# Attention block in float32: another order of the first two pairs, and the bias shift through W1 by column groups

## The chip, the cores and the metric

The kernel runs on one core of one Trainium2 chip, in one launch. Times are device microseconds of that core, medians of several runs; a profile is one further execution, recorded instruction by instruction. Engine names in the text: PE (TensorE), DVE (VectorE), ACT (ScalarE), POOL (GpSimd), SP (the queue that only issues DMAs); PEq, ACTq, SPq are the instruction queues of an engine.

## The reference

A cross-attention block of a transformer, all in float32, for 128 sequences of 128 tokens, 256 features, 16 heads of 16, with an FFN of 1024:

```python
q = query @ Wq + bq;  k = context @ Wk + bk;  v = context @ Wv + bv     # heads of 16
scores = q k^T / 4;  scores[j >= i] = -1e30                              # strictly below the diagonal
attn = softmax(scores);  attn[row 0] = 0
x = layer_norm(query + (attn v) @ Wo + bo, ln1_g, ln1_b)
out = layer_norm(x + relu(x @ W1 + b1) @ W2 + b2, ln2_g, ln2_b)
```

The kernel folds the first norm's gain and shift into the FFN: with x1 the norm without gain and shift, x @ W1 + b1 = x1 @ (g1 * W1) + (b1 + ln1_b @ W1).

## The kernel before, in words

Two sequences are a *pair*; there are 64 pairs. For each the kernel transposes x and the context (`tokens`, a DVE 32x32 transpose of blocks that the load DMAs have already put in place), projects them (`queries`, `keys`, `values`, PE with eviction on ACT), and computes the scores in two parts. "High" (hi = 1) is the second half of the query rows against all 128 keys, "low" (hi = 0) the first half against 64 keys. Each part goes through `mask` (DVE, PSUM to `sm`), `maximum` (DVE reduce `nmx`, then POOL subtracts, L355), `exponential` (ACT), and `sums` (DVE reduce and reciprocal, then POOL multiplies, L376).

The weights are then transposed for the product with the values: `turn` (DVE 32x32 transposes into `tb`) and `bring` (sixteen DMAs tb to pT that exchange the blocks), or `turn_on_pe` (four PE transposes and an ACT copy per piece). `weigh` and `context` give the attention's output (ACT copies it to cxT), `attention_out` multiplies by Wo, `attention_sum`, `attention_stats`, `norm1` make x1. `turn_x1` transposes x1 (DVE, then four DMAs to DRAM, x1t, and one back, x1T); `turn_x1_on_pe` does it with PE and ACT. `hidden` is the first FFN product with ReLU on ACT, `second` the other, `second_sum`, `stats`, `norm2`, `finish`, `store` the last norm and the output. `add_bo`, `residual1`, `scale_and_shift` and `finish` run on POOL.

The order of instructions on every engine is written by hand: each engine executes its instructions in the order of the Python calls, and tiles of a pool hold a writer back until the former readers are done (PSUM: four single banks and two pairs). Nothing is reordered by a scheduler.

The program has four parts: an opening for pairs 0 and 1; steps p = 2 to 6, each in one order with a `plan` that says which halves of the FFN of earlier pairs run where; the usual step `steady(p)` from p = 7 to 62; and an end. In step p the pair p goes through its softmax, pair p-1 through `weigh` to x1, pair p+1 is projected, and the FFN runs for pairs p-2 (`hidden`) and p-3 (`second`). In the usual step the sixteen `bring` DMAs are issued half by SP, half by ACT between the pieces of `hidden`.

Three folds are made on the chip once: `fold_values` (bv @ Wo + bo), `fold_norm1` with `add_b1` (ln1_b @ W1 + b1, a column per 128 hidden units, `b1e_c`), and `scale_w1` (W1 times the gain). `fold_norm1` before is 32 matmuls with 128x128 of W1 as weights and one moving column (`ps_b`, L564).

Of the kernel before, what the change touches and what calls it, by code (L numbers as in the profile page):

```python
# [13 lines left out]
P = 128  # L14
# [5 lines left out]
def tile_cross_attention_block(  # L20
# [107 lines left out]
    c_first = const.tile([P, 2, D], F32, tag="c_first", name="c_first")  # L128
    nc.sync.dma_start(c_first, c[0:2].rearrange("b p d -> p b d"))
# [3 lines left out]
    wv = weight(Wv, "wv")  # L133
    power = const.tile([P, 2, 1], F32, tag="power", name="power")
# [7 lines left out]
    load([1])  # L142
# [6 lines left out]
    load([2, 3], "x")  # L149
    w1 = weight(W1, "w1")  # L150
    load([2, 3], "c")
    load_tokens(0, slice(2, 4))
# [4 lines left out]
    load_tokens(1)  # L157
    g2_r = row(ln2_g, "g2_r")
# [157 lines left out]
    def scores(p, hi):  # L316

        st = states[p]
        n = P if hi else HP
        sps = [pair(f"pss{hi}_{p}_{t}") for t in range(2)]  # L320
        for m in range(KC):
            for s in range(2):
                first = s * P
                for r in range(NS):
                    strip = slice(32 * r, 32 * r + 32)
                    nc.tensor.matmul(  # L326
                        sps[r // 2][
                            s * HP : (s + 1) * HP, r % 2, m * 2 * n : (m + 1) * 2 * n
                        ].rearrange("p (e j) -> p e j", e=2),
                        st["qT"][strip, m, first + hi * HP : first + hi * HP + HP],  # L330
                        st["kT"][strip, m, :, first : first + n],
                        start=True, stop=True,
                    )
# [221 lines left out]

    ps_b1 = None

    def fold_norm1():

        nonlocal ps_b1  # L560
        ps = ps_b1 = bank("ps_b1")
        for f in range(FC):
            for k in range(KC):
                nc.tensor.matmul(  # L564
                    ps[:, f : f + 1], w1[:, k, f * P : (f + 1) * P], be1_c[:, k : k + 1],
                    start=(k == 0), stop=(k == KC - 1),
                )

    def add_b1():
        nc.vector.tensor_tensor(b1e_c, ps_b1[:, :FC], b1_c, ALU.add)  # L570
# [7 lines left out]
    def fold_values():  # L578

        ps = bank("ps_bv")  # L580
        for k in range(KC):
            nc.tensor.matmul(
                ps[:, :D], bvw[:, k, :], wo[:, k, :], start=(k == 0), stop=(k == KC - 1)
            )
        nc.vector.scalar_tensor_tensor(bov_r, ps[:, :D], live, bo_r, ALU.mult, ALU.add)
# [14 lines left out]
    def turn_x1_on_pe(p):  # L600
# [6 lines left out]
        for k in range(KC):  # L607
            nc.scalar.copy(st["x1T"][:, :, :, k, :], pt[:, k])  # L608

    def hidden(p, fs, between=None):  # L610
# [3 lines left out]
        for f in fs[::2]:  # L614
# [25 lines left out]

    def second_alone(p, s):

        st = states[p]
        if "t2" not in st:
            st["t2"] = ffn.tile([P, 2, D], F32, tag="t2", name=f"t2_{p}")
        py = bank(f"py_{p}_{s}")
        for f in range(FC):
            nc.tensor.matmul(  # L648
                py[:, :D], st["hT"][:, f, s * P : (s + 1) * P], w2[:, f, :],
                start=(f == 0), stop=(f == FC - 1),  # L650
            )
        st["py", s] = py

    def sum_alone(p, s):
        st = states[p]
        nc.vector.tensor_tensor(
            st["t2"][:, s], st.pop(("py", s))[:, :D], st["x1b"][:, s], ALU.add
        )
# [17 lines left out]
    for which, first in (("x", tokens_of[0][:, 0:2]), ("c", c_first)):  # L676
# [16 lines left out]
    keys(0)  # L693

    def feed(units):
        for what, p, part in units:
            if what == "hidden":
                hidden(p, range(part * FC // 2, (part + 1) * FC // 2))
            elif p in alone:
                second_alone(p, part)  # L700
            else:
                second(p, part)

    def sum_up(units):

        done = []
        for what, p, part in units:
            if what == "second":
                if p in alone:
                    sum_alone(p, part)  # L710
                elif part == 1:
                    second_sum(p)
                if part == 1:
                    done.append(p)
        return done

    alone = (1, 2)

    def both(what, p):
        return [(what, p, 0), (what, p, 1)]  # L720


    scores(0, 1)
    mask(0, 1, 0)
    maximum(0, 1, ONE)
    values(0)
    mask(0, 1, 1)
    maximum(0, 1, TWO)
    scores(0, 0)
    tokens(1, "x")  # L730
    exponential(0, 1, ONE)
    values_out(0)
    queries(1)
    sums(0, 1, ONE)
    mask(0, 0, 0)
    mask(0, 0, 1)
    tokens(1, "c")
    exponential(0, 1, TWO)
    maximum(0, 0, ALL)
    keys(1)  # L740
    sums(0, 1, TWO)
    values(1)
    exponential(0, 0, ALL)
    turn_on_pe(0, 1, range(2))
    values_out(1)
    sums(0, 0, ALL)
    scores(1, 1)
    mask(1, 1, 0)
    maximum(1, 1, ONE)
    fold_values()  # L750
    turn_on_pe(0, 1, range(2, 4))
    turn_on_pe(0, 0, range(2))
    add_bo(0)
    mask(1, 1, 1)
    maximum(1, 1, TWO)
    tokens(2, "x")
# [3 lines left out]
    fold_norm1()  # L760
    mask(1, 0, 0)
    mask(1, 0, 1)
    exponential(1, 1, ONE)
# [3 lines left out]
    scale_w1()  # L767
    tokens(2, "c")
    add_b1()
# [3 lines left out]
    sums(1, 1, ONE)  # L773
    norm1(0)
    sums(1, 1, TWO)
    exponential(1, 0, ALL)
    keys(2)
    values(2)
    turn_x1_on_pe(0)
    values_out(2)  # L780
    sums(1, 0, ALL)
    for which in "xc":
        tokens(3, which)
    nc.gpsimd.tensor_tensor(be1b_r, be1_r, b2_r, ALU.add)
    residual1(0)
    add_bo(1)
    load([4, 5])
    load_tokens(2)
    add_bo(2)
    feed([("hidden", 0, 0)])  # L790
    turn_on_pe(1, 1, range(4))
    turn_on_pe(1, 0, range(2))

    plan = {
        2: ([("hidden", 0, 1)], both("second", 0), [("hidden", 1, 0)]),
        3: ([("hidden", 1, 1)], [("second", 1, 0)], [("second", 1, 1)]),
        4: ([("hidden", 2, 0)], [("hidden", 2, 1)], [("second", 2, 0)]),
        5: ([("second", 2, 1)], [("hidden", 3, 0)], [("hidden", 3, 1)]),  # L800
    }
# [7 lines left out]
    def steady(p):  # L809

        nonlocal waiting, late
# [3 lines left out]
        second(p - 3, 0)  # L815
# [3 lines left out]
        second(p - 3, 1)  # L819
        if p + 2 < NP:  # L820
            tokens(p + 2, "c")
        sums(p, 1, ONE)
        exponential(p, 1, TWO)
        summed = late + sum_up(both("second", p - 3))
# [6 lines left out]
        queries(p + 1)  # L831
# [6 lines left out]
        for q in waiting:  # L838
            finish(q)
        attention_out(p - 1)  # L840
# [3 lines left out]
        if p + 2 < NP:  # L844
            tokens(p + 2, "x")
        turn(p, 0, 0)
# [3 lines left out]
        turn_x1(p - 1)  # L850
        values(p + 1)
# [11 lines left out]
        def share(f):  # L863
            nonlocal at
            n = 0 if f == 0 else NS if f == FC - 2 else NS // 2
# [3 lines left out]
        hidden(p - 2, range(FC), share)  # L869
        late = []  # L870
# [4 lines left out]
    waiting, late = [], []  # L875
    for p in range(2, NP):
        soon, end = p + 1 < NP, p == NP - 1
        first, then, finally_ = plan.get(
            p, ([("second", p - 3, 0)], [("second", p - 3, 1)], both("hidden", p - 2))
        )  # L880
        load_ahead(p)
        if p > 6 and not end:
            steady(p)
            continue
        scores(p, 1)
        mask(p, 1, 0)
        maximum(p, 1, ONE)
        feed(first)
        mask(p, 1, 1)
        maximum(p, 1, TWO)  # L890
        scores(p, 0)
        mask(p, 0, 0)
        mask(p, 0, 1)
        exponential(p, 1, ONE)
        maximum(p, 0, ALL)
        exponential(p, 1, TWO)
        feed(then)
        sums(p, 1, ONE)
        sums(p, 1, TWO)
        summed = late + sum_up(first + then)  # L900
        exponential(p, 0, ALL)
        sums(p, 0, ALL)
        for q in waiting:
            finish(q)
        weigh(p - 1)
        context(p - 1)
        if soon:
            queries(p + 1)
        attention_out(p - 1)
        if not end:  # L910
            turn(p, 1, 0)
            turn(p, 1, 1)
            turn(p, 0, 0)
            bring(p, nc.sync, range(NS * NS))
        attention_sum(p - 1)
        attention_stats(p - 1)
        if soon:
            keys(p + 1)
        if p + 2 < NP:
            for which in "xc":  # L920
                tokens(p + 2, which)
        norm1(p - 1)
        if p > 4:
            turn_x1(p - 1)
        if soon:
            values(p + 1)
            values_out(p + 1)
        for q in waiting:
            store(q)
        if p == 2:  # L930
            turn_x1_on_pe(p - 1)
        residual1(p - 1)
        for q in summed:
            stats(q, states[q]["t2"], 2)
        if soon:
            add_bo(p + 1)
        for q in summed:
            scale_and_shift(q)
        feed(finally_)
        if end:  # L940
            turn_on_pe(p, 1, range(4))
        if p in (3, 4):
            turn_x1_on_pe(p - 1)
        late = sum_up(finally_)
        for q in summed:
            norm2(q)
        waiting = summed
# [88 lines left out]
```

## Time and profile before

| | us |
|---|---|
| median of 3 runs (lowest, highest) | 1605.69 (1603.98, 1606.11) |
| profiled execution | 1604.26 |
| its span on the core | 1602.5 |
| PE busy in the span | 1581.9 (99%) |
| DVE, POOL, ACT busy | 1368.0, 1281.9, 758.9 |

The profiled execution's own time is 1.8 us above its span. Busy time of PE is that of pipelined matmuls whose ends are modelled, so 99% says that PE is nearly always occupied, not that it is at its peak. Durations in the text come from this one execution.

### The profile page before, as it was taken

How to read it: one execution, taken by the hardware profiler on the slowest of the kernel's cores; microseconds unless marked ns; L12 is line 12 of the kernel's file. 1: busy time of each engine (PE TensorE's matmuls, PEld its weight loads, DVE VectorE, ACT ScalarE, POOL GpSimd, SP SyncE). 2: the span in 40 equal slices, each digit the busy share in tenths (PEclk: the TensorE clock that was granted, in tenths of full speed). 3: DMA queues.
4: the chain of work that ended last, by engine and by line, in shares of the span. 5: the costliest groups of instructions: out<-in, count | busy, mean ns of one | idle time of the engine just before them, and what ended most of it. 6: DMA issues, size and time to landing. Idle time of an engine off the chain costs nothing.

```text
span 1602.5 us, 41277 instructions
## 1 busy us (share of the span) xinstructions
PE 1581.9 (99%) x16532; PEld 1333.4 (83%) x16532; DVE 1368.0 (85%) x1988; ACT 758.9 (47%) x1500; POOL 1281.9 (80%) x1105
## 2 busy tenths in 40 slices
PE   7999999999999999999999999999999999999998
PEld 6788888888888888888888888888888888888887
DVE  5789898898888988988988888888889889889862
ACT  4544444544444545444544444444444455455442
POOL 5688888888888888888888888878888888888882
PEclk9999999999999999999999999999999999999999
DMA  7455656666565566565565565565655665654430
GB/s 179 72 117 126 147 128 141 132 134 146 128 147 132 128 147 146 121 152 133 122 156 138 117 148 129 131 150 128 144 134 133 141 145 127 149 132 107 117 83 27
DMA packets 479999, 208.80 MB, mean 130 GB/s; under 512 B 352064, under 2 KB 448320, under 8 KB 479808
## 3 DMA queue, kind: packets, MB, share of 16 engines
q1 hardware_dynamic: 373360, 137.17, 39.3%
q10 hardware_dynamic: 106448, 68.99, 16.6%
q8 instruction: 131, 2.15, 0.6%
q14 instruction: 60, 0.49, 0.1%
HBM read 69.48 MB, written 32.24 MB: 63 GB/s over the span
## 4 chain that ended last, share of the span: by engine, by line
PE 94%; DVE 3%; POOL 1%; ACT 1%; issue 1%; DMA 1%; ACTq 0%; SPq 0%; POOLq 0%; DVEq 0%
PE ph L618 27%; PE py L636 26%; PE pq L260 7%; PE po L465 7%; PE pk L260 7%; PE pv L292 6%; PE pss L326 6%; PE pc L446 3%; PE pc L436 2%; DVE sm L343 1%; DVE nmx L354 1%; PE py L648 1%; PE ptp L419 0%; POOL sm L376 0%; ACT kT L282 0%
## 5 line engine op out<-in xcount | busy, mean ns | idle before, releaser
L355 POOL TENSOR_TENSOR sm<-sm,nmx 128x1024 f32<-128x1024 f32 x192 | 364.2, 1897 | 135.9 <-DVE nmx L354 135.8
L618 PE MATMUL ph<-x1T,w 128*128 128x256 f32 x2048 | 454.1, 379 | 2.1 <-ACT x1T L608 2.1
L636 PE MATMUL py<-w,hT 128*128 128x256 f32 x1952 | 438.9, 382 | 0.5 <-ACT hT L624 0.5
L618 PEld LDWEIGHTS ph<-x1T,w 128*128 128x128 f32 x2048 | 388.5, 190 | 56.8 <-ACT x1T L608 3.2
L636 PEld LDWEIGHTS py<-w,hT 128*128 128x128 f32 x1952 | 365.6, 190 | 71.1 <-issue 15.5
L376 POOL TENSOR_TENSOR sm<-sm,rs 128x1024 f32<-128x1024 f32 x192 | 364.0, 1898 | 71.7 <-DVE rs L375 68.8
L624 ACT ACTIVATE hT<-ph,b1e_c 128x256 f32<-128x256 f32 x512 | 212.6, 471 | 205.2 <-PE ph L618 127.6
L343 DVE TENSOR_TENSOR sm<-pss,neg 128x1024 f32<-128x1024 f32 (+1 forms) x256 | 235.4, 940 | 78.3 <-PE pss L326 77.1
L362 ACT ACTIVATE sm<-sm 128x1024 f32<-128x1024 f32 x192 | 202.2, 1055 | 206.7 <-POOL sm L355 206.3
L374 DVE TENSOR_REDUCE su<-sm 128x8 f32<-128x1024 f32 (+1 forms) x192 | 233.5, 1216 | 51.1 <-ACT sm L362 47.7
L389 DVE STREAM_TRANSPOSE tb<-sm 128x1024 f32<-128x1024 f32 x183 | 219.8, 1227 | 28.3 <-POOL sm L376 27.7
L354 DVE TENSOR_REDUCE nmx<-sm 128x8 f32<-128x1024 f32 (+1 forms) x192 | 234.2, 1220 | 6.6
L534 ACT ACTIVATE t<-t,nb,sd 128x256 f32<-128x256 f32 x124 | 67.7, 593 | 181.8 <-DMA pT<-tb 110.7
L282 ACT ACTIVATE kT<-pk,bkh,half 128x256 f32<-128x256 f32 x256 | 122.6, 558 | 15.5 <-PE pk L260 15.5
L260 PE MATMUL pq<-xT,wq 128*128 128x256 f32 x512 | 127.9, 393 | 1.2 <-DVE xT L245 1.2
L465 PE MATMUL po<-wo,cxT 128*128 128x256 f32 x512 | 122.9, 383 | 1.4 <-ACT cxT L458 1.4
L260 PE MATMUL pk<-cT,wk 128*128 128x256 f32 x512 | 121.1, 379 | 1.3 <-DVE cT L245 1.3
L326 PE MATMUL pss<-kT,qT 32*64 32x256 f32 (+1 forms) x4096 | 118.1, 334 | 3.0 <-DVE sm L343 1.7
L292 PE MATMUL pv<-wv,cT 128*128 128x256 f32 x512 | 121.1, 379 | 0.0
L271 ACT ACTIVATE qT<-pq,bqs_c 128x256 f32<-128x256 f32 x128 | 53.6, 470 | 122.4 <-PE pq L260 122.4
L513 POOL TENSOR_TENSOR x1b<-x,g_r 128x512 f32<-128x512 f32 x64 | 81.7, 1276 | 36.9 <-DVE x L505 36.9
L465 PEld LDWEIGHTS po<-wo,cxT 128*128 128x128 f32 x512 | 98.2, 192 | 15.1 <-ACT cxT L458 1.6
(86 smaller groups left out, 1780.9 us busy)
## 6 DMA issues: line engine op xcount, KB each, us to landing
pT<-tb SPq DMA_DIRECT2D x528, 96.0 KB, 2.9
pT<-tb ACTq DMA_DIRECT2D x448, 96.0 KB, 2.8
out_dram<-t ACTq DMA_DIRECT2D x63, 256.0 KB, 2.5
xb<-in_x_dram SPq DMA_DIRECT2D x124, 128.0 KB, 4.4
cb<-in_ctx_dram SPq DMA_DIRECT2D x124, 128.0 KB, 4.4
x<-in_x_dram SPq DMA_DIRECT2D x31, 512.0 KB, 5.0
x1t<-tbx SPq DMA_DIRECT2D x236, 64.0 KB, 2.2
x1T<-x1t SPq DMA_DIRECT2D x59, 256.0 KB, 3.3
```

The source lines that it names most:

```text
L260: nc.tensor.matmul(ps[:, m * TP : (m + 1) * TP], w[:, k, m * P : (m + 1) * P], src[:, k, :], start=(k == 0), stop=(k == KC - 1),)
L292: nc.tensor.matmul(pv[:, s * D : (s + 1) * D], st["cT"][:, k, s * P : (s + 1) * P], wv[:, k, :], start=(k == 0), stop=(k == KC - 1),)
L326: nc.tensor.matmul(sps[r // 2][s * HP : (s + 1) * HP, r % 2, m * 2 * n : (m + 1) * 2 * n].rearrange("p (e j) -> p e j", e=2), st["qT"][str ...
L343: nc.vector.tensor_tensor(st["sm", hi][:, part, :].rearrange("p (r n) j -> p r n j", r=2), st["sps", hi][t][:, :, : 4 * n].rearrange("p r ...
L354: nc.vector.tensor_reduce(nmx[:, part], sm[:, part, :], AX.X, ALU.max, negate=True)
L355: nc.gpsimd.tensor_tensor(sm[:, part, :], sm[:, part, :], nmx[:, part, None].to_broadcast([P, part.stop - part.start, n]), ALU.add,)
L374: nc.vector.tensor_reduce(su, sm[:, part, :], AX.X, ALU.add)
L376: nc.gpsimd.tensor_tensor(sm[:, part, :], sm[:, part, :], rs[:, :, None].to_broadcast([P, part.stop - part.start, n]), ALU.mult,)
L389: nc.vector.transpose(st["tb"][:, :, at : at + 256].rearrange("p j (n a) -> p n j a", a=32), st["sm", hi].rearrange("p h j -> p (h j)")[:, ...
L465: nc.tensor.matmul(po[:, s * D : (s + 1) * D], cxT[:, k, s, :], wo[:, k, :], start=(k == 0), stop=(k == KC - 1),)
L618: nc.tensor.matmul(ph[:, i * TP : (i + 1) * TP].rearrange("p (s i a) -> p s i a", s=2, a=32), w1[:, k, (f + i) * P : (f + i + 1) * P], st[ ...
L636: nc.tensor.matmul(st["py"][:, s * D : (s + 1) * D], st["hT"][:, f, s * P : (s + 1) * P], w2[:, f, :], start=(f == 0), stop=(f == FC - 1),)
```

## The change

The opening and the first steps are written in another order.

- Pair 1 is no longer loaded as blocks (`load([1])`) and turned by DVE. Its x and context come as plain tokens, are transposed by PE after `scores(0, 1)`, and copied by ACT. `load([2, 3])` is issued earlier, `load([4, 5])` in the opening.
- `keys(0)` is written out with one bank per 128 outputs; ACT evicts the first, DVE the second.
- The order of calls in the opening differs throughout. `fold_norm1`, the transposes of pair 1's weights and the first half of `hidden(0)` come after `scores(2, 1)` instead of before it, so the high scores tile `sm1` has two buffers.
- `fold_norm1` uses ln1_b as weights of one column and W1 as the moving operand: eight matmuls of 256 columns, four column groups at PSUM partitions 0, 32, 64 and 96. Its result lies along four rows, which ACT copies to `b1s`; `add_b1` brings them into columns with eight DMAs on SP and adds b1 on POOL. This happens in step 2, after `turn_x1(1)`. Until then pair 0 goes through the FFN with the unscaled W1: gain and shift are applied to its x1T by ACT, and `scale_w1` follows `hidden(0)`.
- The usual step, now `step(p)`, runs from p = 2 on. In step 2 the FFN part is `hidden(0)` alone. Pairs 1, 2 and 3 turn x1 with `turn_x1`. The `plan`, `feed`, `second_alone` and `sum_alone` are gone. The end is the same.

```diff
+    load_tokens(0, slice(2, 4))
+    nc.sync.dma_start(c_first[:, 2:4], c[2:4].rearrange("b p d -> p b d"))
-    load([1])
...
-        st["sm", hi] = soft.tile([P, H, n], F32, tag=f"sm{hi}", name=f"sm{hi}_{p}")
+        st["sm", hi] = soft.tile(
+            [P, H, n], F32, tag=f"sm{hi}", name=f"sm{hi}_{p}", bufs=1 + hi
+        )
...
     def fold_norm1():
+        ps = bank("ps_b1")
+        n = DFF // NS
+        for k in range(KC):
+            for j in range(NS):
+                nc.tensor.matmul(
+                    ps[32 * j : 32 * j + 1, :n], be1_c[:, k : k + 1],
+                    w1[:, k, j * n : (j + 1) * n], start=(k == 0), stop=(k == KC - 1),
+                )
+        for j in range(NS):
+            at = slice(32 * j, 32 * j + 1)
+            nc.scalar.copy(b1s[at], ps[at, :n])
+
+    def add_b1():
         for f in range(FC):
-            for k in range(KC):
-                nc.tensor.matmul(
-                    ps[:, f : f + 1], w1[:, k, f * P : (f + 1) * P], be1_c[:, k : k + 1],
-                    start=(k == 0), stop=(k == KC - 1),
-                )
-    def add_b1():
-        nc.vector.tensor_tensor(b1e_c, ps_b1[:, :FC], b1_c, ALU.add)
+            j, u = f // 2, f % 2
+            nc.sync.dma_start(
+                b1e_c[:, f : f + 1], b1s[32 * j : 32 * j + 1, u * P : (u + 1) * P]
+            )
+        nc.gpsimd.tensor_tensor(b1e_c, b1e_c, b1_c, ALU.add)
...
     def turn_x1_on_pe(p):
...
+            if p == 0:
+                nc.scalar.activation(
+                    st["x1T"][:, :, :, k, :], pt[:, k], AF.Identity,
+                    bias=be1_c[:, k : k + 1], scale=g1_c[:, k : k + 1],
+                )
...
     def hidden(p, fs, between=None):
...
-                    bias=b1e_c[:, f + i : f + i + 1], scale=1.0,
+                    bias=(b1e_c if p else b1_c)[:, f + i : f + i + 1], scale=1.0,
...
+    def step(p):
+        if p > 2:
+            load_ahead(p)
         scores(p, 1)
         mask(p, 1, 0)
         maximum(p, 1, ONE)
+        if p > 2:
+            second(p - 3, 0)
+        else:
+            turn_x1_on_pe(0)
+            fold_norm1()
+            turn_on_pe(1, 1, range(4))
+            hidden(0, range(FC // 2))
+            turn_on_pe(1, 0, range(2))
         mask(p, 1, 1)
         maximum(p, 1, TWO)
         exponential(p, 1, ONE)
...
+        else:
+            for which in "xc":
+                tokens(3, which)
+            add_bo(1)
+            load_ahead(2)
+            load_tokens(2)
         sums(p, 1, ONE)
         exponential(p, 1, TWO)
         sums(p, 1, TWO)
         weigh(p - 1)
         context(p - 1)
         scores(p, 0)
         queries(p + 1)
         mask(p, 0, 0)
         mask(p, 0, 1)
         maximum(p, 0, ALL)
         exponential(p, 0, ALL)
         turn(p, 1, 0)
         turn(p, 1, 1)
...
+        if p == 2:
+            nc.gpsimd.tensor_tensor(be1b_r, be1_r, b2_r, ALU.add)
+            residual1(0)
+            add_bo(2)
         attention_out(p - 1)
         attention_sum(p - 1)
         sums(p, 0, ALL)
         attention_stats(p - 1)
...
         turn(p, 0, 0)
         bring(p, nc.sync, range(NS * NS // 2))
         keys(p + 1)
         norm1(p - 1)
         turn_x1(p - 1)
+        if p == 2:
+            add_b1()
         values(p + 1)
         values_out(p + 1)
...
         add_bo(p + 1)
         residual1(p - 1)
...
+        hidden(p - 2, range(0 if p > 2 else FC // 2, FC), share)
+        if p == 2:
+            scale_w1()
```

More of the change, by code (lines that the diff above doesn't have):

```diff
@@ L127, in tile_cross_attention_block @@
     wq = weight(Wq, "wq")
-    c_first = const.tile([P, 2, D], F32, tag="c_first", name="c_first")
-    nc.sync.dma_start(c_first, c[0:2].rearrange("b p d -> p b d"))
+    c_first = const.tile([P, 4, D], F32, tag="c_first", name="c_first")
+    nc.sync.dma_start(c_first[:, 0:2], c[0:2].rearrange("b p d -> p b d"))
     bq_c = column(bq, "bq_c")
@@ L148, in tile_cross_attention_block @@
     be1_c = chunks(ln1_b, "be1_c")
-    load([2, 3], "x")
+    load([2, 3])
     w1 = weight(W1, "w1")
-    load([2, 3], "c")
-    load_tokens(0, slice(2, 4))
     g1_r = row(ln1_g, "g1_r")
@@ L157, in tile_cross_attention_block @@
     load_tokens(1)
+    load([4, 5])
     g2_r = row(ln2_g, "g2_r")
@@ L554, in tile_cross_attention_block @@
     b1e_c = const.tile([P, FC], F32, tag="b1e_c", name="b1e_c")
-    ps_b1 = None
+    b1s = const.tile([P, DFF // NS], F32, tag="b1s", name="b1s")
     def fold_norm1():
-        nonlocal ps_b1
-        ps = ps_b1 = bank("ps_b1")
-        for f in range(FC):
-            for k in range(KC):
-                nc.tensor.matmul(
-                    ps[:, f : f + 1], w1[:, k, f * P : (f + 1) * P], be1_c[:, k : k + 1],
-                    start=(k == 0), stop=(k == KC - 1),
-                )
-    def add_b1():
-        nc.vector.tensor_tensor(b1e_c, ps_b1[:, :FC], b1_c, ALU.add)
+        ps = bank("ps_b1")
[10 more added lines that the diff above has]
+    def add_b1():
+        for f in range(FC):
+            j, u = f // 2, f % 2
[3 more added lines that the diff above has]
+        nc.gpsimd.tensor_tensor(b1e_c, b1e_c, b1_c, ALU.add)
     def scale_w1():
@@ L584, in fold_values, with add_values @@
             )
+        return ps
+    def add_values(ps):
         nc.vector.scalar_tensor_tensor(bov_r, ps[:, :D], live, bo_r, ALU.mult, ALU.add)
@@ L607, in turn_x1_on_pe @@
         for k in range(KC):
-            nc.scalar.copy(st["x1T"][:, :, :, k, :], pt[:, k])
+            if p == 0:
[4 more added lines that the diff above has]
+            else:
+                nc.scalar.copy(st["x1T"][:, :, :, k, :], pt[:, k])
     def hidden(p, fs, between=None):
@@ L639, in second @@
             )
[L641 to L658, printed above, removed]
     def second_sum(p):
@@ L675, in tile_cross_attention_block @@
     states[0] = {}
-    for which, first in (("x", tokens_of[0][:, 0:2]), ("c", c_first)):
+    for which, first in (("x", tokens_of[0][:, 0:2]), ("c", c_first[:, 0:2])):
         st = states[0]
@@ L692, in tile_cross_attention_block @@
     queries(0)
[L693 to L700, printed above, removed]
-            else:
[L702 to L715, printed above, removed]
@@ L717, in tile_cross_attention_block @@
-    alone = (1, 2)
-    def both(what, p):
-        return [(what, p, 0), (what, p, 1)]
-    scores(0, 1)
+    st["kT"] = proj.tile([P, KC, 2, TP], F32, tag="kT", name="kT_0")
+    for m in range(KC):
+        pk = bank(f"pk_0_{m}")
+        for k in range(KC):
+            nc.tensor.matmul(
+                pk[:, :TP], wk[:, k, m * P : (m + 1) * P], st["cT"][:, k, :],
+                start=(k == 0), stop=(k == KC - 1),
+            )
+        for e in range(2):
+            if m == 0:
+                nc.scalar.activation(
+                    st["kT"][:, m, e, :], pk[:, :TP], AF.Identity,
+                    bias=bkh[:, m, e : e + 1], scale=half[:, e : e + 1],
+                )
+            else:
+                nc.vector.tensor_scalar(
+                    st["kT"][:, m, e, :], pk[:, :TP], half[:, e : e + 1],
+                    bkh[:, m, e : e + 1], ALU.mult, ALU.add,
+                )
@@ L724, in tile_cross_attention_block @@
+    scores(0, 1)
+    states[1] = {}
+    for which, first in (("x", tokens_of[0][:, 2:4]), ("c", c_first[:, 2:4])):
+        st = states[1]
+        st[which + "T"] = proj.tile([P, KC, TP], F32, tag=which + "T", name=f"{which}T_1")
+        pt = transposed(first, f"pt{which}_1")
+        nc.scalar.copy(st[which + "T"].rearrange("p k i -> p (k i)"), pt)
+    values(0)
+    values_out(0)
     mask(0, 1, 0)
     maximum(0, 1, ONE)
-    values(0)
     mask(0, 1, 1)
     maximum(0, 1, TWO)
+    exponential(0, 1, ONE)
@@ L729, in tile_cross_attention_block @@
+    queries(1)
     scores(0, 0)
[L730 to L734, printed above, removed]
     mask(0, 0, 0)
     mask(0, 0, 1)
-    tokens(1, "c")
+    maximum(0, 0, ALL)
     exponential(0, 1, TWO)
-    maximum(0, 0, ALL)
+    sums(0, 1, ONE)
     keys(1)
     sums(0, 1, TWO)
+    exponential(0, 0, ALL)
     values(1)
-    exponential(0, 0, ALL)
-    turn_on_pe(0, 1, range(2))
-    values_out(1)
+    ps_bv = fold_values()
     sums(0, 0, ALL)
@@ L748, in tile_cross_attention_block @@
     mask(1, 1, 0)
+    add_values(ps_bv)
     maximum(1, 1, ONE)
-    fold_values()
+    turn_on_pe(0, 1, range(2))
+    values_out(1)
     turn_on_pe(0, 1, range(2, 4))
-    turn_on_pe(0, 0, range(2))
-    add_bo(0)
     mask(1, 1, 1)
     maximum(1, 1, TWO)
-    tokens(2, "x")
+    add_bo(0)
+    turn_on_pe(0, 0, range(2))
+    for which in "xc":
+        tokens(2, which)
     weigh(0)
@@ L759, in tile_cross_attention_block @@
     scores(1, 0)
-    fold_norm1()
+    exponential(1, 1, ONE)
     mask(1, 0, 0)
     mask(1, 0, 1)
-    exponential(1, 1, ONE)
     maximum(1, 0, ALL)
@@ L766, in tile_cross_attention_block @@
     exponential(1, 1, TWO)
-    scale_w1()
-    tokens(2, "c")
-    add_b1()
     attention_sum(0)
@@ L773, in tile_cross_attention_block @@
     sums(1, 1, ONE)
+    keys(2)
     norm1(0)
+    exponential(1, 0, ALL)
     sums(1, 1, TWO)
-    exponential(1, 0, ALL)
-    keys(2)
     values(2)
-    turn_x1_on_pe(0)
     values_out(2)
     sums(1, 0, ALL)
[L782 to L801, printed above, removed]
     def load_ahead(p):
@@ L807, in load_ahead @@
             load_tokens((p + 3) // 2)
-    def steady(p):
-        nonlocal waiting, late
+    def step(p):
+        nonlocal waiting
+        soon = p + 1 < NP
+        if p > 2:
+            load_ahead(p)
         scores(p, 1)
@@ L814, in steady @@
         maximum(p, 1, ONE)
-        second(p - 3, 0)
+        if p > 2:
[6 more added lines that the diff above has]
+            turn_on_pe(1, 0, range(2))
         mask(p, 1, 1)
@@ L818, in steady @@
         exponential(p, 1, ONE)
-        second(p - 3, 1)
-        if p + 2 < NP:
-            tokens(p + 2, "c")
+        summed = []
+        if p > 2:
+            second(p - 3, 1)
+            if p + 2 < NP:
+                tokens(p + 2, "c")
+        else:
+            for which in "xc":
+                tokens(3, which)
+            add_bo(1)
+            load_ahead(2)
+            load_tokens(2)
         sums(p, 1, ONE)
         exponential(p, 1, TWO)
-        summed = late + sum_up(both("second", p - 3))
+        if p > 2:
+            second_sum(p - 3)
+            summed = [p - 3]
         sums(p, 1, TWO)
@@ L830, in steady @@
         scores(p, 0)
-        queries(p + 1)
+        if soon:
+            queries(p + 1)
         mask(p, 0, 0)
@@ L845, in steady @@
             tokens(p + 2, "x")
+            if p == 2:
+                tokens(p + 2, "c")
         turn(p, 0, 0)
@@ L864, in share @@
             nonlocal at
-            n = 0 if f == 0 else NS if f == FC - 2 else NS // 2
+            n = 0 if f == 0 else NS * NS - at if f == FC - 2 else NS // 2
             bring(p, nc.scalar, range(at, at + n))
             at += n
-        hidden(p - 2, range(FC), share)
-        late = []
+        hidden(p - 2, range(0 if p > 2 else FC // 2, FC), share)
+        if p == 2:
+            scale_w1()
         for q in summed:
@@ L873, in steady @@
         waiting = summed
[L875 to L947, printed above, removed]
@@ new lines, in tile_cross_attention_block @@
+    waiting = []
+    for p in range(2, NP - 1):
+        step(p)
+    p = NP - 1
+    scores(p, 1)
+    mask(p, 1, 0)
+    maximum(p, 1, ONE)
+    second(p - 3, 0)
+    mask(p, 1, 1)
+    maximum(p, 1, TWO)
+    scores(p, 0)
+    mask(p, 0, 0)
+    mask(p, 0, 1)
+    exponential(p, 1, ONE)
+    maximum(p, 0, ALL)
+    exponential(p, 1, TWO)
+    second(p - 3, 1)
+    sums(p, 1, ONE)
+    sums(p, 1, TWO)
+    second_sum(p - 3)
+    exponential(p, 0, ALL)
+    sums(p, 0, ALL)
+    finish(p - 4)
@@ L949, in tile_cross_attention_block @@
+    weigh(p - 1)
+    context(p - 1)
+    attention_out(p - 1)
+    attention_sum(p - 1)
+    attention_stats(p - 1)
+    norm1(p - 1)
+    turn_x1(p - 1)
+    store(p - 4)
+    residual1(p - 1)
+    stats(p - 3, states[p - 3]["t2"], 2)
+    scale_and_shift(p - 3)
+    hidden(p - 2, range(FC))
+    turn_on_pe(p, 1, range(4))
+    norm2(p - 3)
     p = NP - 1
```

## The prediction

> **What bounds the kernel now.** I read the page first, then the busy time by stretches, the chain of waits in order of time, and the timeline of the first 175 us and of two late steps. The page:
>
> ```profile
> PE 1581.9 (99%) x16532; PEld 1333.4 (83%) x16532; DVE 1368.0 (85%) x1988; ACT 758.9 (47%) x1500; POOL 1281.9 (80%) x1105
> ...
> DVE  5789898898888988988988888888889889889862
> ...
> L355 POOL TENSOR_TENSOR sm<-sm,nmx 128x1024 f32<-128x1024 f32 x192 | 364.2, 1897 | 135.9 <-DVE nmx L354 135.8
> ...
> L376 POOL TENSOR_TENSOR sm<-sm,rs 128x1024 f32<-128x1024 f32 x192 | 364.0, 1898 | 71.7 <-DVE rs L375 68.8
> ```
>
> PE is the bound, but DVE (85%) and POOL (80%, two instructions of 1.9 us making most of it) have little room: a late POOL can't be hidden for long. By stretches (PE, PEld, DVE, ACT, POOL busy, then the granted clock, DMA share, GB/s):
>
> ```profile
> 29.60:36.40 6.80, 5.80 (x157) 5.14 (x157) 6.70 (x9) 3.08 (x5) 4.96 (x4) 1.00 0.54 121
> 36.40:43.20 6.80, 6.80 (x23) 5.94 (x23) 2.50 (x4) 3.24 (x3) 2.44 (x2) 0.50 0.94 233
> ...
> 400.00:1400.00 1000.00, 999.47 (x10636) 844.31 (x10636) 888.94 (x1279) 478.97 (x946) 824.56 (x699) 1.00 0.59 137
> ```
>
> In the usual step PE never rests; one stretch at half clock lies at 36.4 to 43.2. The chain (start, length, what):
>
> ```profile
> 34.15 4.82 PE ps_b L564 x32
> 38.97 3.62 PE po L465 x8
> ...
> 55.54 1.16 PE pss L326 x32
> ...
> 95.56 1.73 PE po L465 x8
> ...
> 173.51 1.05 PE pss L326 x32
> ...
> 185.69 1.73 PE po L465 x8
> ...
> 197.77 1.05 PE pss L326 x32
> ```
>
> 55.54 is `scores(2, 1)`, 95.56 `attention_out(2)`, 173.51 `scores(7, 1)`, 197.77 `scores(8, 1)`: a usual step is 24.26 us, and 12.08 us from its `attention_out` to the next step. At `scores(7, 1)` both kernels have done the same pairs and go on, and end, in the same order. So the change is worth what it moves this one time, 173.51.
>
> Last, the tail of one usual step in the timeline, and landings from the list of DMAs (KB, us):
>
> ```profile
> 433.95 1.90 POOL L376 TENSOR_TENSOR sm<-sm,rs 128x1024 f32<-128x1024 f32 x1 [0.18 <-DVE rs L375]
> ...
> 435.89 1.25 DVE L389 STREAM_TRANSPOSE tb<-sm 128x1024 f32<-128x1024 f32 x1 [0.45 <-POOL sm L376]
> ...
> 437.20 6.03 SPq L404 DMA_DIRECT2D pT<-tb  x8
> ...
> 443.34 2.21 SPq L237 DMA_DIRECT2D x1t<-tbx  x4
> ...
> 446.96 0.38 SPq L240 DMA_DIRECT2D x1T<-x1t  x1
> ```
>
> ```profile
> x1t<-tbx SPq DMA_DIRECT2D x236, 64.0 KB, 2.2
> x1T<-x1t SPq DMA_DIRECT2D x59, 256.0 KB, 3.3
> ...
> be_c<-in_L_xattn_ln_b_dram ACTq DMA_DIRECT2D x1, 1.0 KB, 3.5
> ```
>
> From the start of the low half's turn to the issue of x1T, SP needs 446.96 - 435.89 = 11.1 us. This is the queue that the new shift goes behind.
>
> **The change, part by part.**
>
> *Keys of pair 0.* Four kT evictions on ACT in a row took 1.93; now two lie beside the second projection and two go to DVE (0.38 each, by the 128x256 PSUM add of L656). `scores(0, 1)` ends at 11.7 instead of 12.74.
>
> *Pair 1 on TensorE.* Adds 8 transposes (0.66 per four, 1.3) on PE and two ACT copies (0.58 each, by the cxT copy); removes two DVE transposes (0.70 each) and eight load DMAs (6 us of SP's issuing), and the waits of `pq` and `pk` for them (1.2 and 1.3). The two 256 KB loads that replace them are asked for at about 4 us, and 7 us remain: hidden.
>
> *Order up to `scores(2, 1)`.* Walking the new order with the durations above, POOL's last multiply of pair 0 ends at 27.1 (was 30.13), the ACT copies for `weigh(0)` at 29.2 (was 31.95), `scores(1, 0)` starts at 31.0 (was 33.53). ps_b (4.82) no longer stands before `attention_out(0)`, which starts at 31.7 instead of 38.97. `queries(2)`, `keys(2)`, `values(2)` at 1.73 each end at 38.7; ACT gives kT (37.1 to 39.0) and then the low exponential of pair 1 (to 40.05); DVE sums it until 41.5 and takes the first mask of pair 2. Call that moment M: 41.5 (was 57.16). PE still waits here for pair 0's softmax, with little but transposes from 22 to 29, so I take the half clock to come again; in the trace it cost half of 6.8, 3.4. Part will lie on waits: M = 44.0 (41.5 to 44.9).
>
> *What the clock does.* The row says that PE was gated after a stretch in which it was busy 5.80 of 6.80 us, and for 6.8 us. The Trainium skill (TensorE: Matmul & The Clock Gate, "What's actually happening") has it gated after a whole idle window of some 3.4 us and freed after one busy window. By that rule alone M would be 41.5 and the sum below 2.5 less; the row decides.
>
> *High weights twice buffered.* Without it the first mask of pair 2 would have to wait for the transposes of pair 1, which now come later. No cost but memory; in the usual step the previous turn is long done.
>
> *Step 2 in the usual order.* ACT first: after the exponential, the values (1.8), x1T (0.8, now with scale and shift), four ps_b copies (1.4, by the 0.35 of L302), four ptp copies (2.1), four hT (1.7) and two more ptp copies (1.1), each waiting a little for banks: the exponentials of pair 2 start at M+8.65. DVE sums them until M+11.2 and 12.6; POOL multiplies until M+15.0, subtracts the low maximum until 17.0, and then has four instructions that stood elsewhere before (be1b_r 0.7, residual1(0) 2.55, add_bo(2) 1.27): 21.5, low multiply until 23.4. The low turn starts at M+23.45. PE has 21 us of work here and waits for others; what it loses is already in these numbers. The eight ps_b matmuls (0.5 to 1.7, four column groups) lie beside the ACT copies.
>
> *The shift through SP.* The eight copies b1s to b1e_c are issued after the turn's eight, four x1t and x1T: x1T at M+23.45+11.1 = 34.5. The eighth of them reuses the semaphore of x1T, so it waits for that landing (3.3): issued at M+37.9. Its own landing isn't in the trace: between 2.2 (x1t) and 3.5 (be_c, the only row that scatters 4-byte pieces); I take 2.4, SBUF to SBUF being nearest to the first: M+40.3. POOL's add (L581 there) waits for all eight. Queued behind it on POOL, in order: add_bo(3) 1.27, residual1(1) 2.55, and **both subtractions of step 3's maximum**. POOL was free at M+24.35: it stands for 16 us. Who waits: subtractions end at M+46.3 and 48.2, ACT's exponentials at 49.2, the cxT copy of `context(2)`, which is behind them on ACT, at 49.8, and so `attention_out(2)` starts at M+50. PE would be there at M+38.2 (weigh(2) at 34.3, when ACT's last eight pT copies have landed, then 1.5, scores 0.7, queries 1.7): 12 us of idle PE.
>
> The Trainium skill (DMA: Bandwidth & Descriptors, "Rules for kernel authors") speaks against this shift: join small transfers, since below 64 KB one pays mostly overhead. These are 512 bytes each; one in their place would by the rows above go out at M+34.9 and land at 37.3, 3 us earlier, with the same wait behind the turn.
>
> **The sum.** `attention_out(2)` at 44.0+50.0 = 94.0. Then 12.1 to the next step, three steps of 24.26 (72.8): 178.9. Added: 1.5 because DVE and POOL come out of the stall some 2 us behind the usual step, whose low turn has no room (its last pT landing and `weigh` fall together at 448.5), and 1.7, half of the possible 3.4, for a clock that 12 us of idling will have halved. 182.1 against 173.5: 8.6 later. The gains are all in it: before, the same pairs at 95.56 had 10.4 us more of FFN behind them (three halves of 3.45). Profiled 1604.26 becomes 1612.9; the median of the runs is 1.4 above the profiled run, so 1614. Bounds: M 41.5, landing 2.2, no lag, no second half clock: +2.4 (1608). M 44.9, landing 3.5, lag 4, clock 3.4: +15 (1621).
>
> **Rivals.**
>
> *The wait hides (faster).* If the shift lands by about M+28, POOL goes on as in the usual step, exponentials follow scale_w1 on ACT at M+34, and `attention_out(2)` starts at M+38.2. `scores(7, 1)` is then at 38.2+84.9+M = 164.6 to 167.1 (M 41.5 to 44): 6 to 9 us gained, 1598. For it: PE's saved work is real (ps_b shrinks by some 3.5, four fewer transposes), and in before the five steps from 55.5 to 173.5 take 118.0 where their parts (17 halves of 3.45, five times 10.4 for the rest, three x1 transposes of 0.6) sum to 112.5. Against it: the SP rows above; the turn would have to be 12 us earlier. It decides at po(2) = 85, break-even with the lag left out at 88.6.
>
> *Even.* Landing and SP issue 3 us quicker and no half clock in either place: within 0.2%, 1605.
>
> *Slower than forecast.* The lag isn't regained: in the usual step DVE has only 11% to spare, 2.7 us a step, and ACT's pT copies land as `weigh` starts. If 2 more us are lost in each of steps 4 to 6, both half clocks come whole and the copies land in 3.5: 44.9+51.1+84.9+7.5+3.4 = 191.8, +18, 1623.
>
> **How the numbers follow.** Forecast 0.70 (own range 1608 to 1621), hidden 0.14, even 0.08, much slower 0.08. About 0.2%, 3.2 us, is what a measurement tells from no change. The forecast's low end adds 0.02 to no change. Faster 0.14, same 0.10, slower 0.76. The range 1603 to 1622 leaves out the first rival and part of the last.
>
> **What would show it.** POOL idle some 16 us before the new 128x8 add, released by a DMA from b1s; PE idle some 12 us before po of pair 2, released by ACT cxT; `scores(2, 1)` near 40 to 43; `scores(7, 1)` near 182; 24.26 us a step afterwards. Wrong if POOL's add finds its data there, or if the exponentials of step 3 start before M+40; if `scores(7, 1)` is right and the end is not, the equal rest is the error.

## The result and the profile after

The changed kernel took 1615.76 us (median of 4 runs, 1615.05 to 1616.84) beside 1605.9 of the kernel before on the same chip: ratio 1.006, 95% interval 1.0042 to 1.0078, so slower by 0.4 to 0.8%. The profiled execution took 1615.05, its span 1613.3. Forecast were 1614 us (1603 to 1622), with a chance of 0.76 for slower.

The page of after, engines, granted clock by slices, and one group (busy, mean ns | idle before, releaser):

```profile
PE 1579.5 (98%) x16512; PEld 1330.4 (82%) x16512; DVE 1370.9 (85%) x1988; ACT 755.9 (47%) x1498; POOL 1282.6 (79%) x1106
...
PEclk9979999999999999999999999999999999999999
...
L467 PE MATMUL po<-wo,cxT 128*128 128x256 f32 x512 | 123.0, 384 | 16.2 <-ACT cxT L460 16.1
```

PE does less (1579.5 for 1581.9 before) and the program is longer. One clock digit in the third slice and one group's idle time point at a single place, `attention_out(2)`. The timeline there (start, length, engine; in brackets the idle time before, and its releaser), queue by queue:

```profile
66.67 7.10 SPq L406 DMA_DIRECT2D pT<-tb  x8
73.86 2.01 SPq L237 DMA_DIRECT2D x1t<-tbx  x4
79.16 0.38 SPq L240 DMA_DIRECT2D x1T<-x1t  x1
79.59 5.07 SPq L578 DMA_DIRECT2D b1e_c<-b1s  x8
...
86.50 0.20 POOL L581 TENSOR_TENSOR b1e_c<-b1e_c,b_c 128x8 f32<-128x8 f32 x1 [20.27 <-DMA b1e_c<-b1s]
...
92.36 1.06 ACT L364 ACTIVATE sm<-sm 128x1024 f32<-128x1024 f32 x1 [17.99 <-POOL sm L357]
...
95.79 3.78 PE L467 MATMUL po<-wo,cxT 128*128 128x256 f32 x8 [14.69 <-ACT cxT L460]
```

Read from below: PE has stood 14.69 us for the cxT copy, which stands on ACT behind the exponentials of pair 3, which waited 17.99 for POOL's subtraction, and POOL had stood 20.27 us before a 0.20 us addition, for copies that SP could issue only behind the turn. The chain of waits goes through the same stations and then runs in equal steps:

```profile
84.06 2.05 DMA b1e_c<-b1s
...
90.48 3.71 POOL sm L357 x2
...
95.79 3.78 PE po L467 x8
...
110.40 1.05 PE pss L326 x32
...
134.66 1.05 PE pss L326 x32
...
183.19 1.05 PE pss L326 x32
```

`scores(7, 1)` is at 183.19 where before had 173.51: 9.7 of the 10.8 us by which the spans differ. The other 1.1 lies after it (1430.1 for 1429.0), in a stream of equal instructions that took from 1428.8 to 1431.6 in the seven experiments.

### The profile page after: what moved, and what is told of

Its sections match the earlier page's. It is cut to its first block, busy times and chain, and to the rows that moved or that the text cites. A ratio compares the mean times of both kernels' runs of the same rounds, so it can differ in the third digit from the quotient of the medians.

```text
span 1613.3 us, 41269 instructions
## 1 busy us (share of the span) xinstructions
PE 1579.5 (98%) x16512; PEld 1330.4 (82%) x16512; DVE 1370.9 (85%) x1988; ACT 755.9 (47%) x1498; POOL 1282.6 (79%) x1106
## 4 chain that ended last, share of the span: by engine, by line
PE 94%; POOL 2%; DVE 2%; DMA 1%; SPq 1%; ACT 1%; issue 0%; POOLq 0%; ACTq 0%; DVEq 0%
PE ph L639 27%; PE py L657 26%; PE pq L260 7%; PE po L467 7%; PE pv L292 7%; PE pk L260 7%; PE pss L326 6%; PE pc L448 3%; PE pc L438 2%; POOL sm L357 1%; DVE sm L345 0%; POOL sm L378 0%; DVE nmx L356 0%; PE ptp L421 0%; DMA x1t<-tbx 0%
## 5 line engine op out<-in xcount | busy, mean ns | idle before, releaser
L657 PE MATMUL py<-w,hT 128*128 128x256 f32 x2016 | 453.2, 382 | 1.8 <-ACT hT L645 1.7
L657 PEld LDWEIGHTS py<-w,hT 128*128 128x128 f32 x2016 | 377.6, 190 | 75.1 <-issue 19.0
L645 ACT ACTIVATE hT<-ph,b1e_c 128x256 f32<-128x256 f32 x504 | 208.4, 471 | 210.3 <-PE ph L639 107.3
L260 PEld LDWEIGHTS pq<-xT,wq 128*128 128x128 f32 x512 | 92.7, 191 | 21.0 <-issue 10.8
```

The lines of the kernel that those rows point to most:

```text
L260: nc.tensor.matmul(ps[:, m * TP : (m + 1) * TP], w[:, k, m * P : (m + 1) * P], src[:, k, :], start=(k == 0), stop=(k == KC - 1),)
L657: nc.tensor.matmul(st["py"][:, s * D : (s + 1) * D], st["hT"][:, f, s * P : (s + 1) * P], w2[:, f, :], start=(f == 0), stop=(f == FC - 1),)
```

## The experiments

Each ratio is to runs of the kernel before on the same chip: median 1605.9 beside after, 1605.6 beside the next four rows, 1606.0 beside the last three. The three columns at the right are starts in each profiled execution: of `keys(0)` in the timeline of PE, of the other two in the chain of waits.

| | median us (runs) | ratio to before, 95% | keys(0) | attention_out(2) | scores(7, 1) |
|---|---|---|---|---|---|
| after | 1615.8 (4) | 1.0042 to 1.0078 | 7.74 | 95.79 | 183.19 |
| add late | 1598.5 (8) | 0.9954 to 0.9977 | 10.15 | 82.68 | 167.56 |
| old fold | 1600.0 (11) | 0.9961 to 0.9986 | 9.97 | 82.88 | 167.76 |
| copies twice | 1619.2 (4) | 1.0086 to 1.0114 | 8.76 | 99.67 | 187.10 |
| copies early | 1602.6 (11) | 0.9978 to 0.9999 | 10.87 | 87.96 | 172.84 |
| copies after loads | 1604.6 (12) | 0.9976 to 1.0 | 10.35 | 87.48 | 172.36 |
| POOL behind | 1599.2 (6) | 0.9935 to 0.9966 | 10.40 | 80.08 | 166.11 |
| one buffer | 1601.1 (7) | 0.9954 to 0.9981 | 8.92 | 84.69 | 169.57 |

Up to `keys(0)` all eight kernels run the same instructions, yet the starts differ by up to 3.1 us. PE begins at half clock, at which a matmul of `queries(0)` takes 0.63 us, and 0.38 afterwards. The trace's records of the clock begin when it is freed: at 4.8 to 5.4 us in after, copies twice and one buffer, at 9.5 to 11.0 in the other five. Besides, PE waited 0.49 us for the first context in after and 0.99 to 1.65 in the experiments. So 1 to 3 us between two rows of these columns can come from the opening alone. Counted from `keys(0)`, the late add moves `scores(7, 1)` by 18.0, not by the 15.6 of the column.

### The add alone moved

The theory is that POOL's place in the queue is the loss, not the work of the change. So the eight copies stay where they are on SP, and only the waiting instruction moves, behind the sums of the low half of step 3. `copy_b1` now holds the eight DMAs, `add_b1` the addition alone:

```diff
         sums(p, 0, ALL)
+        if p == 3:
+            add_b1()
...
         if p == 2:
-            add_b1()
+            copy_b1()
```

> The eight copies stay where they are on SP; only POOL's add moves, behind the multiply of step 3's low half. Theory (the wait of POOL's queue is the loss): POOL goes on at 66.2 instead of 86.5, the subtractions of step 3 end near 74.6, ACT is free of scale_w1 at 74.4, and attention_out(2) starts when PE has done queries(4), near 80 instead of 95.8; the half clock of 83 to 100 (2.5 us on PE) goes too. 1598 us, some 17.5 below the changed kernel and 8 below the kernel before. Rival 1 (the late pT copies and SP's queue hold step 3 anyway): weigh(2) and what follows stay, at most 5 us are won, 1611 or more. Rival 2 (the usual step is too dense to run from step 2 on, DVE and POOL lag): the stall goes but comes back as waits in steps 4 to 6, 1606 to 1612.

Measured 1598.5, faster than both kernels, by 0.23 to 0.46% than before. The timeline of this kernel:

```profile
79.29 5.08 SPq L578 DMA_DIRECT2D b1e_c<-b1s  x8
...
89.54 0.21 POOL L584 TENSOR_TENSOR b1e_c<-b1e_c,b_c 128x8 f32<-128x8 f32 x1
...
82.51 1.89 PE L467 MATMUL po<-wo,cxT 128*128 128x256 f32 x8
```

The copies take what they took. The add has no bracket: it waited for nothing. The product starts at 82.51, again without a bracket. Moving one 0.2 us instruction is worth 17 us (1615.8 to 1598.5), and the rest of the change is worth 7 (1605.6 to 1598.5). The product comes 2.5 us later than the 80 expected. The half clock doesn't go altogether: in this kernel it lies from 77.8 to 81.2, and `weigh(2)` to the end of `queries(4)` take 5.7 us, where they take 4.1 at full clock (in the experiment POOL behind).

### The old fold in the new order

Is the form of the shift (column groups, rows, copies) worth anything, or is all in the order? Here the new order keeps the old fold: 32 matmuls into columns, added by DVE from PSUM, no copies, no wait on POOL.

```diff
-        for k in range(KC):
-            for j in range(NS):
+        for f in range(FC):
+            for k in range(KC):
                 nc.tensor.matmul(
-                    ps[32 * j : 32 * j + 1, :n], be1_c[:, k : k + 1],
-                    w1[:, k, j * n : (j + 1) * n], start=(k == 0), stop=(k == KC - 1),
+                    ps[:, f : f + 1], w1[:, k, f * P : (f + 1) * P], be1_c[:, k : k + 1],
+                    start=(k == 0), stop=(k == KC - 1),
                 )
...
-        nc.gpsimd.tensor_tensor(b1e_c, b1e_c, b1_c, ALU.add)
+        nc.vector.tensor_tensor(b1e_c, ps[:, :FC], b1_c, ALU.add)
```

> The new order with the old shift: 32 matmuls of one moving column and the add on DVE from PSUM, behind the maximum of the first high half of step 2; no copies on SP, no wait on POOL. Theory: the stall goes as with the late add, and PE has 32 x 0.11 to 0.15 = 3.5 to 4.8 us of ps_b instead of 1.0, in a stretch that ACT sets, where ACT has 1.5 us less to copy: 1600 us (1597 to 1603). If the new form of the matmuls is worth its own 3 us, this is 3 above the late add; if ACT covers it, the two are equal. Rival 2 (lag): 1606 to 1612.

Measured 1600.0. `ps_b` takes 3.63 us on PE here and 1.04 with column groups, but the place after `scores(2, 1)` has room beside ACT, and the two intervals (0.9961 to 0.9986, 0.9954 to 0.9977) overlap. The gain is the order's. That the column groups are worth anything when their result isn't waited for is not shown: the medians differ by 1.5 us, which these runs don't resolve. As the change has them, waited for, they cost 16 (1600.0 to 1615.8).

### The copies twice

If SP's issuing and the landing price the stall, eight more copies (into a tile that nobody reads, before the real ones) must lengthen it by their issue time.

```diff
-        for f in range(FC):
-            nc.sync.dma_start(b1e_c[:, f : f + 1], ...)
+        for to in (b1d, b1e_c):
+            for f in range(FC):
+                nc.sync.dma_start(to[:, f : f + 1], ...)
```

> The eight copies are issued twice, first into a tile that nobody reads, then as in the changed kernel. In the trace one costs SP 0.64 us, so the add comes 8 x 0.64 = 5.1 us later. Theory: everything behind it comes 5.1 us later, 1620.9 us, or a little more if the half clock covers more of what follows. Rivals 1 and 2 (the wait is not what ends last): no change, 1615.8.

```profile
90.37 0.20 POOL L584 TENSOR_TENSOR b1e_c<-b1e_c,b_c 128x8 f32<-128x8 f32 x1 [23.95 <-DMA b1e_c<-b1s]
```

The addition waits 23.95 instead of 20.27, and `scores(7, 1)` is 3.9 later; the time is 3.5 longer, not the 5 expected. The eight extra copies took 5.44 on SP, but x1T went out 1.7 earlier this time (77.50, as the x1t copies before it landed sooner): the eight that count went out 3.8 later (83.41 for 79.59), the add 3.9. The stall follows SP's queue one to one.

### The copies early, in two places

The other way to cure it is to issue the copies earlier and leave the add in its place. First, right behind the first half of pair 1's low transposes in step 2 (`add_b1`, the addition alone, stays where it was):

```diff
             turn_on_pe(1, 0, range(2))
+            copy_b1()
```

> POOL's add stays in its place; the eight copies are issued on SP right after the transposes of pair 1, before the loads of pairs 6 and 7, so they have landed near 52, 14 us before the add. Theory: as with the late add, 1598 us; both moves take the same wait away. Rival 1 (it is SP's queue that is late, not POOL's wait): this one wins, since x1T and the next loads are followed by 5 us less on SP, and the late add does not. Rival 2 (lag): 1606 to 1612, as with the late add.

Measured 1602.6, where 1598 was expected: a miss. POOL no longer stands (the add runs at 68.80 without a wait), but 4 of the 7 us are lost. The list of SP's waits between 50 and 75 us names one (total, count, longest):

```profile
SPq L100 <- DMA pT<-tb: 17.3, 1, 17.3
```

L100 is `load_tokens(2)`, the tokens of pairs 4 and 5, which have nothing to do with pT. In the program the DMAs of SP and ACT take their completion semaphores from one set of eight in turn, in an order that is fixed when the program is built, and each waits until the last user of its semaphore has landed. The trace names them: numbers 100 to 103 and 105 to 108, used by both queues. In this order the load got number 106, which a pT copy has before it that ACT issues only at 69.14. SP's half of the turn stands behind that load and starts at 72.08 (68.24 with the add moved), and `weigh(2)` waits 6.5 us. To test this, the copies go behind that load:

```diff
             turn_on_pe(1, 0, range(2))
-            copy_b1()
...
             load_ahead(2)
             load_tokens(2)
+            copy_b1()
```

> The eight copies of the shift are issued in step 2 behind the loads of pairs 6 and 7 (behind load_ahead(2) and load_tokens(2)) instead of before them; the add stays where the change puts it. Theory of the miss of the early copies: there, the token load behind them waited 17.3 us for a pT copy of ACT's queue and held SP's half of the turn back by some 4 to 5 us; the copies themselves are free that early, and POOL finds its data. Then the load goes out near 52.5, the copies at 53 to 58.5, SP is free before the turn at 68.2, weigh(2) is back at 77.0 to 77.5, attention_out(2) near 82.5: 1598.5 (1597 to 1600.5), as with the add alone moved. Rival: small copies issued before the turn cost its transfers time wherever they stand; then it stays at 1602 to 1603 with weigh(2) near 82.

Measured 1604.6: a miss. The load does go out at once (52.54), but the copies take its place as the waiting ones. Timeline and SP's waits:

```profile
56.15 18.38 SPq L578 DMA_DIRECT2D b1e_c<-b1s  x8
74.71 5.52 SPq L406 DMA_DIRECT2D pT<-tb  x8
...
SPq L578 <- DMA vd<-vz: 10.3, 1, 10.3
...
SPq L578 <- DMA pT<-tb: 3.1, 1, 3.1
SPq L578 <- DMA xb<-in_x_dram: 3.0, 1, 3.0
```

Eight copies that took 5.07 us one after another lie over 18.38, waiting for transfers of other tiles, two of the three kinds issued by ACT. SP comes to the turn 6.5 us later than with the add moved, and `weigh(2)` waits 7.1. POOL's add waits again, 8.97 us until 77.12, but `attention_out(2)` doesn't wait for what follows it: PE runs from `weigh(2)` to it without a rest. My theory that the place before the load was to blame falls; these lists show what both have in common: a DMA on SP waited for the transfer that used its semaphore before, on either queue (the second copy has number 106, which vd<-vz has before it, issued by ACT at 64.27), and on SP it held all behind it.

### POOL's four instructions behind the turn

On top of the add moved: be1b_r, residual1(0) and add_bo(2), 4.55 us that stand before the low multiply of step 2, go behind the low turn.

```diff
-        if p == 2:
-            nc.gpsimd.tensor_tensor(be1b_r, be1_r, b2_r, ALU.add)
-            residual1(0)
-            add_bo(2)
         attention_out(p - 1)
...
         turn(p, 0, 0)
+        if p == 2:
+            nc.gpsimd.tensor_tensor(be1b_r, be1_r, b2_r, ALU.add)
+            residual1(0)
+            add_bo(2)
         bring(p, nc.sync, range(NS * NS // 2))
```

> On top of the add moved to step 3: the four instructions that POOL has in front of the low multiply of step 2 (be1b_r 0.73, the two of residual1(0) 1.27 each, add_bo(2) 1.28: 4.55 in all) are issued behind the low turn. Theory, that they delay the turn and with it the context of pair 2: DVE's sums give rs at 63.1 in the kernel with the late add, the multiply then starts there instead of 64.9, so the turn, SP's copies and weigh(2), which waits 2.49 for them, come 1.8 earlier: 1596.8 (1595.5 to 1598). Rival: ACT's half of the turn is issued between the pieces of hidden(0) and is tied to norm1(1), not to POOL; then weigh(2) stays at 77.0 and the time at 1598.5, or the later residuals delay POOL's subtractions of step 3 and cost 1 to 2 us: 1600.

```profile
63.49 1.91 POOL L378 TENSOR_TENSOR sm<-sm,rs 128x1024 f32<-128x1024 f32 x1 [2.77 <-DVE rs L377]
...
75.74 0.46 PE L438 MATMUL pc<-pT,vd 128*32 128x64 f32 x16 [2.49 <-DMA x1t<-tbx]
```

The multiply starts 1.4 us earlier than with the add alone moved (64.91) and is now held by DVE; `weigh(2)` comes 1.3 earlier, `scores(7, 1)` 1.45. Not all of that is the move's: the clock stays full here behind `weigh(2)`, which alone is worth 1.5 (5.7 for 4.1, as above). What the rival named is there too: the subtractions of step 3 start 2.0 later (74.71 for 72.69), and `attention_out(2)` waits 0.22 us for the cxT copy that comes behind them on ACT; `weigh(3)` then waits 0.80 for the transposed weights (pT). The whole time shows no gain, and its median lies above the expected range: 6.8 us under before, where the add alone moved gave 7.1, each against its own runs of before. The profiled spans are equal (1596.5, 1596.4), since the stream after `scores(7, 1)` took 1.5 longer in this one. So the turn comes earlier, as meant, and that this is worth anything is not shown.

### One buffer of high weights

Also on top of the add moved:

```diff
-            [P, H, n], F32, tag=f"sm{hi}", name=f"sm{hi}_{p}", bufs=1 + hi
+            [P, H, n], F32, tag=f"sm{hi}", name=f"sm{hi}_{p}"
```

> On top of the add moved to step 3: one buffer of high weights instead of two. The prediction held that the first mask of pair 2 then waits for the transposes of pair 1 and that the second buffer has no other worth. With the late add these transposes end near 46.0 and the mask starts at 43.9: M moves by 2.2, all later instructions of DVE with it, and what of it reaches attention_out(2) is 1 to 2.5 us: 1600.3 (1599.3 to 1601.5). Rival: it is hidden, as DVE rests 2.7 us before the sums of pair 2 at 52.6; then 1598.5 within 0.8.

Measured 1601.1; against before it gains 5.0 where two buffers gain 7.1. Timeline of DVE:

```profile
27.25 1.23 DVE L345 TENSOR_TENSOR sm<-pss,neg 128x1024 f32<-128x1024 f32 x1 [2.33 <-PE ptp L421]
...
48.51 1.23 DVE L345 TENSOR_TENSOR sm<-pss,neg 128x1024 f32<-128x1024 f32 x1 [2.16 <-PE ptp L421]
```

The second line is the wait that the prediction named, and its 2.2 us are as expected. The first it had not seen: pair 1's first mask already waits for pair 0's transposes. PE then lacks work, and in this kernel its clock is at half from 28.7 to 35.6 us. Counted from `keys(0)`, which started 1.2 earlier than with the add alone moved, M (the first mask of pair 2) comes 5.9 later, and 3.2 of it are left at `scores(7, 1)`, as DVE and ACT had rests in step 2. The time lies in the expected range, but by luck in part: 2.2 at M were expected.

## Why the prediction was right, by its own steps

*The mechanism held link by link.* POOL stands before the shift's addition (forecast 16 us, found 20.3), the two subtractions of step 3 stand behind it, then the exponentials, the cxT copy, and PE (forecast 12 us, found 14.7). The late add shows that this is the cause and not only a chain: without it all links are gone.

*The opening, to a few tenths, in part by luck.* Forecast and found: `scores(0, 1)` ends 11.7 and 11.4; `attention_out(0)` 31.7 and 31.60; `values(2)` ends 38.7 and 38.8; ps_b 0.5 to 1.7 and 1.04. The middle two were walked without the half clock and found with it, 0.8 us of it, as shown next; and this execution had the earliest `keys(0)` of the eight.

*M: taken 44.0, found 42.30.* The term that was mis-sized is the half clock in the opening: taken 2.5, it cost 0.8. The clock was halved there in this execution, over the transposes from 25.3 to 28.7. In six of the seven experiments this stretch ran at full clock. The timeline of after, where eight transposes take 1.97 us and the low mask of pair 1 waits 1.75:

```profile
26.74 1.97 PE L421 MATMUL ptp<-ident,sm 128*128 128x128 f32 x8 [0.25 <-POOL sm L378]
...
31.68 1.29 DVE L345 TENSOR_TENSOR sm<-pss,neg 128x512 f32<-128x512 f32 x2 [1.75 <-PE pss L326]
```

The same two lines with the add alone moved, at full clock:

```profile
29.14 1.09 PE L421 MATMUL ptp<-ident,sm 128*128 128x128 f32 x8 [0.77 <-POOL sm L378]
...
33.27 1.29 DVE L345 TENSOR_TENSOR sm<-pss,neg 128x512 f32<-128x512 f32 x2 [0.93 <-PE pss L326]
```

The mask waits 0.82 longer at half clock, and M shows all of it: it comes 34.56 after the start of `keys(0)` in after and 33.73 to 33.79 in the six at full clock. Without the gate M would have been 41.5, the walk's own figure: it had `values(2)` 0.8 later than full clock gives and the way from there to M, where DVE worked without a rest, 0.8 too short. But `keys(0)` came later in those six, so M is at 42.49 to 44.66 there: how far 44.0 is off depends on the execution. The windows of after (PE busy, ..., granted clock, DMA share, GB/s), the stretch before the gate first:

```profile
21.80:25.20 3.40, 1.70 (x27) 1.18 (x12) 2.95 (x6) 1.89 (x5) 3.40 (x3) 1.00 0.78 249
25.20:28.60 3.40, 3.15 (x16) 2.46 (x13) 3.37 (x4) 2.06 (x5) 3.34 (x2) 0.51 1.15 333
...
83.30:95.80 12.50, 0.01 (x1) 0.01 (x1) 2.32 (x4) 2.64 (x4) 8.36 (x7) 0.50 0.41 84
95.80:100.50 4.70, 4.70 (x11) 3.80 (x12) 4.63 (x7) 0.68 (x2) 4.23 (x3) 0.51 0.01 3
```

The clock was halved after a stretch with PE busy for half of it and no rest over 0.94 us. The prediction weighed this row against the Trainium skill (TensorE: Matmul & The Clock Gate, "What's actually happening": gated after a wholly idle window of some 3.4 us). On when the gate comes, the row was nearer, since PE was never idle that long here; on the sum, the page's number was, 0 against 2.5 where 0.8 was found. In the 14.7 us of real idling the clock was halved from 83.3, 2.2 us after PE's last matmul (81.1), so again before 3.4 us had passed, and until 100.4, 4.6 us past the restart.

*From M to the addition: forecast 40.3, found 44.2.* This is the largest error, and nearly all of it is on SP. The turn started 0.5 earlier than forecast (M+22.97). From there to the issue of x1T it took 13.9, not the 11.1 of the usual step: eight pT copies 7.10 for 6.03, and x1T waited 3.1 for the x1t copies to land, where the usual step had 1.2. Then the copies: I let the first seven go out within the 3.3 us of x1T's landing and the eighth wait for it. They were issued at 0.60 to 0.64 us each, the eighth 4.9 after x1T, so the landing hid behind the issuing. Their own landing was 2.05 (taken 2.4, bounds 2.2 to 3.5: below the lower bound), and 0.4 more passed before the add ran.

*From the addition to `attention_out(2)`: 9.7 forecast, 9.3 found.* So `attention_out(2)` came at M+53.5, 95.79, where 94.0 was forecast: 1.7 of M too much and 3.5 of SP too little.

*The second half clock: taken 1.7, found 2.5.* po took 3.78 for 1.73 and pk about 0.45 more.

*The lag: taken 1.5, found none.* From 95.79 to 110.40 are 14.6, the usual 12.1 and the 2.5 of the clock; the three steps to 183.19 are 24.26 each.

In all 1.7 too much, 3.5 too little, 0.8 too little, 1.5 too much: 182.1 became 183.2. With 1.1 in the equal rest and a median 0.7 above the profiled run (1.4 taken), 1614 became 1615.8. The sum was better than its terms. Two of its side sums are off by little and carry nothing: the lowest terms add up to 2.7 above before, not 2.4, and the slowest case to 1624, not 1623.

*The rivals.* "The wait hides" was priced at 1598 us, with `scores(7, 1)` between 164.6 and 167.1 and the decision at po(2) = 85. The late add is this rival built: 1598.5, 167.6, 82.7. Its price was right, its condition was not met. "Even" needed the copies issued and landed 3 us quicker: the copies landed 0.35 quicker, but the whole way from M to the add took 3.9 longer. The rival of a lag that isn't regained fell with the lag.

*Small transfers.* The prediction cited the Trainium skill's advice to join them (DMA: Bandwidth & Descriptors, "Rules for kernel authors"). Copies twice gives the price that it is about, 0.6 to 0.7 us of issuing for 512 bytes (eight in 5.44); a single joined copy wasn't tried. The same section has another rule, to issue a DMA early and wait for it late. The runs price the halves apart: waiting late was worth 17 us here, issuing early without it 13 and 11 (1602.6 and 1604.6 against 1615.8), less because there DMAs had waits of their own.

## What to carry to other kernels

On an engine that works in order, look not at what an instruction costs but at what it waits for and who stands behind it: a 0.2 us addition whose result is first read 19 us after it (by ACT's ReLU at 105.7) belongs close to its use. Before moving DMAs forward, look up what each of them waits for, its semaphore's last user on any queue included, and which transfers stand behind it. Price a row of small DMAs by the issuing queue first and by the landing second.

## What the runs showed of the hardware

A DMA of 512 bytes that spreads one row over 128 partitions cost SP 0.56 to 0.60 us to issue in the changed kernel, 0.64 from one start to the next, as much as one of 96 KB in the same queue (0.5 to 0.6 without its waits), and landed 2.0 to 2.1 us later. In the other kernels it landed in 2.0 to 3.2. The clock of PE can be halved after a stretch in which PE was busy for half of the time with short rests, in one execution and not in another of the same instructions: the transposes of pair 0's weights and what lies beside them, 21 to 29 us in after, were gated there and not in six of the seven experiments, which have the same instructions up to there and run them 1.0 to 3.2 us later. The gate, 3.4 us long, cost 0.8. The half clock of the start was left at 4.8 to 5.7 us in four of the nine executions, after transposes alone, and at 9.5 to 11.0 in the other five.
